# Experts' last layer as seven block products summed over the experts in PSUM, with a new order of layers and a new prologue

## The chip, the core and the metric

The kernel runs on one core of a Trainium2 chip. The metric is the device time of one execution in microseconds (us). Before the change the median of three runs was 1530.85 us (1530.27 to 1532.34). The core has five engines that matter here: PE does matmuls (PEld is its weight load), DVE and ACT do elementwise work, POOL (GpSimd) does some elementwise work and starts some transfers, and SP only starts transfers. PE writes its results to PSUM, which has eight banks of 512 numbers of four bytes for each of 128 partitions.

## The reference

The input x has 32 series of 128 steps with 256 features, that is 4096 tokens of 256. All numbers are 32-bit floats.

```python
# layer 0: attention over all 4096 tokens (8 heads of 32), masked by step
x = _L0_conv_ref(x, ...)            # h + alpha * (softmax(QK/sqrt(hd)) V @ out_w.T + out_b)
# layer 1
t = _to_tokens(x)
t = t + _L1_attn_ref(_ln_t(t), ...) # attention in a window of 24 tokens
t = t + _L1_ffn_ref(_ln_t(t), ...)
...
def _L1_ffn_ref(x, ...):
    feat = jnp.mean(x, axis=0)
    w = jax.nn.softmax(feat @ Wr + br, axis=-1)          # one share per token and expert
    h = jnp.einsum('bfd,edh->bfeh', x, W1) + b1
    h = jax.nn.relu(_bn(h, g1, be1, m1, v1))
    h = jnp.einsum('bfeh,ehk->bfek', h, W2) + b2
    h = jax.nn.relu(_bn(h, g2, be2, m2, v2))
    y = jnp.einsum('bfeh,ehd->bfed', h, Wo) + bo
    return jnp.einsum('bfed,fe->bfd', y, w)              # sum of 8 experts by their shares
```

There are 8 experts. Each has three matrices of 256x256: W1, W2 and Wo. The change concerns the product with Wo and the sum over experts.

## The kernel before, in words

`fast_kernel` has four stages in time. The prologue (to about 21 us) loads and transposes weights and the first tokens, and projects queries and keys. Block attention (to about 733 us) works on scores, exponentials and their products with the values. A transition (to about 777 us) finishes the attention of the last block and does the window attention of the first tokens. The experts' stage takes the rest.

The experts' stage goes through 64 items: 8 blocks of 512 tokens, and 8 experts for each block (`work`, a list of pairs of block and expert). The tokens of a block lie transposed: features on partitions, 512 tokens along a row. For an item, `Layer(0, ...)` multiplies them by W1 and `Layer(1, ...)` by W2, each followed by a relu on ACT with a scale and a shift.

From item 3 on (`PLAIN`) a layer is not the plain product of 2x2 blocks, which takes eight products of 128x128 by 128x256. It takes seven, in the manner of Strassen and Winograd. For this the weights' sums of blocks are computed once for each expert by `weight_sums` on POOL, written to memory (`kept`) and loaded again for later items (tile `s`). The tokens' sums of blocks are computed by `token_sums` on DVE (tiles `tx` for the first layer, `th` for the second). `Layer.first` issues four of the seven products into two PSUM tiles, `a` and `q`, then copies one half of `a` to `u` on ACT (L1960) and makes three additions on DVE (L1961, L1962, L1963). `Layer.last` issues the other three products (the first of them into `a`, two into `q`), then a relu on ACT, one addition on DVE (L1976) and two more relus. Tiles of `ps_h` (four banks) hold `a` and `q` of two layers at a time.

`combine` multiplies by Wo: for half of a block, four plain matmul pairs put tokens on partitions again (tile `psy`, L1991, from a `ps_x` bank), and two DVE instructions (L1999) multiply by the token's share and add to `tokens`, the result in SBUF. When the last expert of a block has been added, the tokens are written out.

The order in the loop over items is written out by hand: first half of the first layer of item k+1, a half combine, first half of the second layer of item k, last half of that first layer, another half combine, last half of that second layer. After each of these, `insert` puts in up to three jobs of later blocks (project, normalise, turn, window attention, route, expert shares). A job is put in when a planner's clock `now`, which adds fixed costs, says that what it needs is 3.2 us old (`LATER`), and when the work already spent is behind a line of due times (`dues`, from `SPAN`).

All 4096 tokens' x are loaded and kept in SBUF from an early time; `with_bias` (L904) adds the output bias on POOL. Tile dependencies hold for whole tiles: a matmul that writes one half of a bank waits for readers of the other half as well.

In the prologue, a tile `stack` gathers eight small vectors by POOL's DMA queue (L1079), is transposed (L1111) and copied to `colT` (L1114); `wsc` (L1116) scales the query weights by one of its columns, after which mean, spread, queries and keys follow up to the first scores, `sa`.

In the transition, `three_a`, `three_b`, `one_a`, `one_b` are PSUM tiles of attention's score pool. It is closed and `ps_h` and `ps_x` are opened in its banks (`open_banks`); the first layers' plain products are at L1939.

Of the kernel before, what the change touches and what calls it, by code (L numbers as in the profile page):

```python
# [16 lines left out]
P = 128  # L17
# [806 lines left out]
def fast_kernel(ctx: ExitStack, tc: tile.TileContext, ins: dict, out: bass.AP, narrow):  # L824
# [101 lines left out]
    with ExitStack() as l0:  # L926
# [73 lines left out]
        def project_q(b, g, hT, ps):  # L1000
# [3 lines left out]
            for c in range(2):  # L1004
# [6 lines left out]
            nc.vector.tensor_tensor(  # L1011
                qv, qv, cq[:, g, :].unsqueeze(1).to_broadcast([P, BLK // N, N]), op=ALU.add
            )
# [41 lines left out]
        with tc.tile_pool(name="pw", bufs=1) as pw, tc.tile_pool(  # L1055
            name="ptr", bufs=8, space=PSUM
        ) as ptr:
            def banks(name, n):
# [11 lines left out]
            nc.gpsimd.memset(onesm, 1.0 / D)  # L1070
            xblk[0] = load_x(0, "xg", (
                lambda: nc.scalar.dma_start(out=wQ_n, in_=in_w[0]),
                lambda: nc.scalar.dma_start(
                    out=wq_n, in_=ins["L0_conv_wq"].rearrange("(c p) d -> p c d", p=P)
                ),
# [33 lines left out]
            for c in range(2):  # L1109
                ps = ptr.tile([P, BLK], F32, tag="tr", name=f"ps_st{c}")  # L1110
                nc.tensor.transpose(  # L1111
                    ps[:, : NROW + N], stack[:, c * P : (c + 1) * P], ident[: NROW + N, : NROW + N]
                )
                nc.vector.tensor_copy(colT[:, c, :], ps[:, : NROW + N])  # L1114
            for ci in range(2):
                nc.scalar.mul(wsc[:, ci, :], pswc[ci], colT[:, ci, 0:1])  # L1116
            hT = transposed_x(0, banks("pst0", 2))
            for ci in range(2):
                nc.vector.tensor_copy(wraw[:, ci, :], pswc[ci])
            for i in range(TPB):  # L1120
                stats(0, i, xblk[0])
            transposed(wKT, wk_n, "ps_wK", banks, True)
# [6 lines left out]
            for ci in range(2):  # L1129
                nc.vector.tensor_tensor(wcT[:, ci, :], wsc[:, ci, :], ps, op=ALU.subtract)  # L1130

# [8 lines left out]
            def query_bias(g):  # L1140
# [10 lines left out]
                )  # L1151

            query_bias(0)
# [5 lines left out]
            project_q(0, 0, hT, banks("psq0_0", 1)[0])  # L1159
            project_k(0, 0, hT, banks("psk0_0", 1)[0])  # L1160
# [68 lines left out]
        with ExitStack() as at:  # L1229
# [4 lines left out]
            ps_a = scores_ps.enter_context(tc.tile_pool(name="ps_a", bufs=1, space=PSUM))  # L1234
            ps_b = scores_ps.enter_context(tc.tile_pool(name="ps_b", bufs=2, space=PSUM))
            ps_av = scores_ps.enter_context(tc.tile_pool(name="ps_av", bufs=1, space=PSUM))
# [285 lines left out]
    res = ctx.enter_context(tc.tile_pool(name="res", bufs=1))  # L1522
# [7 lines left out]
    ps_h = ps_x = None  # L1530

    def open_banks():
        nonlocal ps_h, ps_x
        scores_ps.close()
        ps_h = ctx.enter_context(tc.tile_pool(name="ps_h", bufs=4, space=PSUM))
        ps_x = ctx.enter_context(tc.tile_pool(name="ps_x", bufs=4, space=PSUM))
# [8 lines left out]
    w12, s12, wo, kept_sums = {}, {}, {}, {}  # L1545
# [15 lines left out]
    def load_last(k):  # L1561
        wo[k] = wf.tile([P, 2, D], F32, tag="wo", name=f"wo_{k}")
        expert_weights(wo[k], "Wo", work[k][1])

    def weight_sums(e):

        t = s12[e] = wf.tile([P, 4, 2, P], F32, tag="s12", name=f"s12_{e}")
        a11, a21, a12, a22 = (
            w12[e][:, :, c, m * P : (m + 1) * P] for c in range(2) for m in range(2)
        )  # L1570
        for k, (p, q, op) in enumerate((
            (a21, a22, ALU.add), (t[:, 0], a11, ALU.subtract),
            (a11, a21, ALU.subtract), (a12, t[:, 1], ALU.subtract),
        )):
            nc.gpsimd.tensor_tensor(t[:, k], p, q, op=op)
        kept_sums[e] = wdr.tile([P, 4, 2, P], F32, name=f"kept{e}")
        nc.sync.dma_start(out=kept_sums[e], in_=t)

    Ksb = l1c.tile([P, 2, D], F32, name="Ksb")
    nc.sync.dma_start(out=Ksb, in_=ins["L1_attn_K"].rearrange("(c p) e -> p c e", p=P))  # L1580
    load_tokens(4, res.tile([P, TPB, D], F32, name="tokens4"))
# [14 lines left out]
    def load_rest():  # L1596
        load_tokens(TPB + 1, res.tile([P, TPB, D], F32, name=f"tokens{TPB + 1}"))
        load_layers(1)
        for b in range(TPB + 2, NBLK):
            load_tokens(b, res.tile([P, TPB, D], F32, name=f"tokens{b}"))  # L1600
# [30 lines left out]
    def project(n):  # L1631
        ps = bank(f"pso{n}")[:, :D]
        for c in range(2):
            project_half(n, c, ps, not c)
        finish(n, ps)
        if n + TPB < NTILE:
            with_bias(n + TPB)
# [157 lines left out]

    def expert_tokens(b, r2):
# [40 lines left out]
    def turn_route(b):  # L1837
# [3 lines left out]
        wide = fx.tile([P, TPB, HD], F32, tag="w", name=f"w{b}")  # L1841
        nc.gpsimd.memset(wide, 0.0)
# [20 lines left out]
    def turn_shares(b):  # L1863
        ps = bank(f"pswt{b}")[:, :P]
        nc.tensor.transpose(ps, blk[b]["wide"].rearrange("p r e -> p (r e)"), ident)
        blk[b]["wT"] = fx.tile([P, P], F32, tag="wT", name=f"wT{b}", bufs=1)
        nc.vector.tensor_copy(blk[b]["wT"], ps)
# [38 lines left out]
    def token_sums(x, tag, name):  # L1906

        t = fh.tile([P, 4, HB], F32, tag=tag, name=name)
        nc.vector.tensor_tensor(
# [3 lines left out]
        nc.vector.tensor_tensor(t[:, 2], x[:, 1, HB:], t[:, 0], op=ALU.subtract)  # L1913
        nc.vector.tensor_tensor(t[:, 3], x[:, 1, :HB], t[:, 2], op=ALU.subtract)
# [8 lines left out]
    class Layer:  # L1923


        def __init__(self, l, k, x, t):
            self.l, self.k, self.x, self.t = l, k, x, t
            self.w, self.s = w12[k][:, l], None if t is None else s12[k][:, :, l]

        def bank(self, m):  # L1930
            return ps_h.tile([P, 2, HB], F32, tag="h", name=f"psh{self.l}_{self.k}_{m}")

        def product(self, ps, w, x, start):
            nc.tensor.matmul(ps, lhsT=w, rhs=x, start=start, stop=True, skip_group_check=True)  # L1934

        def plain(self, m):
# [6 lines left out]
            relu(self.out[:, m, :], ps, self.l, work[self.k][1], m)  # L1943

        def first(self):
            x, t, w, s = self.x, self.t, self.w, self.s
            self.out = fh.tile([P, 2, BLK], F32, tag=f"h{self.l}", name=f"h{self.l}_{self.k}")
# [6 lines left out]
            self.product(a[:, 0], w[:, 0, :P], x[:, 0, :HB], True)  # L1954
# [517 lines left out]
```

## Time and profile before

| | us |
|---|---|
| median of 3 runs | 1530.85 |
| profiled execution | 1529.69 |
| its span, first to last instruction | 1527.6 |
| experts' stage (777 to the end) | 750.6 |
| PE busy / DVE / ACT / POOL | 1477.8 / 1199.8 / 938.0 / 164.7 |
| PE busy from 1400 to 1520 | 119.14 of 120 |

The granted clock of PE was 0.996 over the span, and 0.90 between 777 and 800 us. The page's rows that the change touches most (line, engine, operation, tiles, count, busy us, mean ns of one, idle time of the engine ahead of them):

```profile
L1991 PE MATMUL psy<-wo,h 128*128 128x256 f32 x1024 | 242.9, 380 | 0.0
L1999 DVE SCALAR_TENSOR_TENSOR tokens<-psy,w,tokens 128x256 f32<-128x256 f32 x256 | 111.0, 475 | 34.9 <-PE psy L1991 34.5
L1934 PE MATMUL psh<-tx,s 128*128 128x256 f32 x366 | 89.3, 380 | 0.0
L1976 DVE TENSOR_TENSOR h<-psh,u 128x512 f32<-128x512 f32 x122 | 83.0, 681 | 1.5 <-PE psh L1934 1.4
```

A row is read so: 512 matmuls by Wo show as 1024 records, two for each; records overlap, so their sum is more than the time they take, and the pitch from one matmul to the next has to be read from a timeline.

### The profile page before, as it was taken

What the parts mean: (1) busy time and instruction counts of PE and PEld (TensorE: products, weight loads), DVE (VectorE), ACT (ScalarE), POOL (GpSimd) and SP (SyncE); (2) the same over time, 40 slices, a digit from 0 to 9 for tenths busy, and PEclk for the clock granted to TensorE, in tenths of its full rate; (3) what the DMA queues carried; (4) which work ended last, traced back from release to release, by engine and by line L of the source; (5) the groups of instructions that cost most, each with busy time, mean ns of one, the idle gap of its engine ahead of it and who ended that gap; (6) DMA issues with size and microseconds to landing.
All of it is one profiled execution on the core that took longest, in us unless ns stands there. A gap on an engine that the chain in (4) does not pass through costs nothing.

```text
span 1527.6 us, 23827 instructions
## 1 busy us (share of the span) xinstructions
PE 1477.8 (97%) x8873; PEld 836.2 (55%) x8873; DVE 1199.8 (79%) x2193; ACT 938.0 (61%) x1400; POOL 164.7 (11%) x387
## 2 busy tenths in 40 slices
PE   8999999999999999999989999999999999999998
PEld 5333232222222222222547878887877888888887
DVE  4677879888899898999737777687877877777775
ACT  4676777878888887988545345445454444544443
POOL 2110003000000000031062103001010000000000
PEclk9999999999999999999999999999999999999999
DMA  5211101010000010000323334433433333343442
GB/s 127 48 43 26 29 8 31 8 30 8 1 15 8 2 49 15 8 9 1 116 81 106 103 118 126 127 111 107 130 113 115 123 107 119 119 130 110 138 152 64
DMA packets 96106, 110.16 MB, mean 72 GB/s; under 512 B 17677, under 2 KB 84960, under 8 KB 95984
## 3 DMA queue, kind: packets, MB, share of 16 engines
q1 hardware_dynamic: 93280, 106.87, 23.2%
q8 instruction: 72, 1.18, 0.3%
q0 software_dynamic: 1888, 0.91, 0.2%
q10 hardware_dynamic: 816, 0.79, 0.2%
q14 instruction: 50, 0.41, 0.1%
HBM read 98.87 MB, written 8.53 MB: 70 GB/s over the span
## 4 chain that ended last, share of the span: by engine, by line
PE 75%; DVE 12%; ACT 7%; issue 4%; POOL 1%; DMA 0%; DVEq 0%; ACTq 0%; POOLq 0%
PE psh L1934 18%; PE sa L1271 15%; PE av L1315 14%; PE psy L1991 11%; DVE acc L1305 3%; ACT h L1919 2%; PE psv L1020 2%; PE psq L1005 2%; ACT pt L1285 2%; PE psk L992 2%; PE psk L1685 2%; PE sb L1271 1%; PE sums L1342 1%; PE psh L1939 1%; DVE h L1976 1%
## 5 line engine op out<-in xcount | busy, mean ns | idle before, releaser
L1305 DVE TENSOR_TENSOR acc<-acc,pt 128x1024 f32<-128x1024 f32 (+3 forms) x500 | 529.3, 1126 | 40.6 <-ACT pt L1285 28.4
L1285 ACT ACTIVATE pt<-sb 128x1536 f32<-128x1536 f32 (+3 forms) x288 | 387.3, 1345 | 3.8 <-PE sb L1271 3.6
L1271 PE MATMUL sa<-q,kT 32*128 32x512 f32 (+3 forms) x576 | 302.3, 604 | 9.4 <-ACT pt L1283 7.1
L1271 PE MATMUL sb<-q,kT 32*128 32x512 f32 (+3 forms) x1728 | 306.8, 605 | 1.8 <-ACT pt L1285 0.7
L1919 ACT ACTIVATE h<-h,bshift,bscale 128x256 f32<-128x256 f32 x244 | 159.2, 699 | 228.8 <-DVE h L1976 228.8
L1315 PE MATMUL av<-pt,v 128*32 128x512 f32 (+3 forms) x2304 | 287.0, 571 | 1.5 <-ACT big_t L1330 0.4
L1991 PE MATMUL psy<-wo,h 128*128 128x256 f32 x1024 | 242.9, 380 | 0.0
L1283 ACT ACTIVATE pt<-sa 128x512 f32<-128x512 f32 (+3 forms) x288 | 162.5, 564 | 94.5 <-PE sb L1271 63.1
L1991 PEld LDWEIGHTS psy<-wo,h 128*128 128x128 f32 x1024 | 191.9, 190 | 30.7 <-issue 5.8
L1271 PEld LDWEIGHTS sa<-q,kT 32*128 32x128 f32 x576 | 84.3, 183 | 220.7 <-ACT pt L1283 179.5
L1315 PEld LDWEIGHTS av<-pt,v 128*32 128x32 f32 x2304 | 45.5, 108 | 200.7 <-issue 183.4
L1999 DVE SCALAR_TENSOR_TENSOR tokens<-psy,w,tokens 128x256 f32<-128x256 f32 x256 | 111.0, 475 | 34.9 <-PE psy L1991 34.5
L1961 DVE TENSOR_TENSOR u<-psh,u 128x256 f32<-128x256 f32 x122 | 51.0, 418 | 101.3 <-ACT u L1960 101.0
L1289 POOL MEMSET pt<- 32x128 f32 (+2 forms) x192 | 58.5, 305 | 631.6 <-ACT pt L1285 536.1
L1919 ACT ACTIVATE h<-psh,bshift,bscale 128x256 f32<-128x256 f32 (+1 forms) x132 | 75.9, 575 | 54.7 <-PE psh L1934 41.5
L1960 ACT COPY u<-psh 128x256 f32<-128x256 f32 x122 | 44.2, 362 | 80.3 <-PE psh L1934 80.2
L1271 PEld LDWEIGHTS sb<-q,kT 32*128 32x128 f32 x1728 | 88.1, 183 | 9.1 <-ACT pt L1285 5.8
L1934 PE MATMUL psh<-tx,s 128*128 128x256 f32 x366 | 89.3, 380 | 0.0
L1934 PE MATMUL psh<-th,s 128*128 128x256 f32 x366 | 88.9, 379 | 0.0
L1976 DVE TENSOR_TENSOR h<-psh,u 128x512 f32<-128x512 f32 x122 | 83.0, 681 | 1.5 <-PE psh L1934 1.4
L1934 PEld LDWEIGHTS psh<-tx,s 128*128 128x128 f32 x366 | 69.2, 190 | 10.4 <-DVE h L1976 0.8
L1934 PEld LDWEIGHTS psh<-th,s 128*128 128x128 f32 x366 | 69.5, 190 | 9.5
(329 smaller groups left out, 1771.0 us busy)
## 6 DMA issues: line engine op xcount, KB each, us to landing
w<-in_L_ffn_W_dram SPq DMA_DIRECT2D x128, 256.0 KB
s<-kept SPq DMA_DIRECT2D x56, 512.0 KB
wo<-in_L_ffn_Wo_dram SPq DMA_DIRECT2D x64, 256.0 KB
xg<-in_x_dram SPq DMA_DIRECT2D x32, 128.0 KB
tokens<-in_x_dram SPq DMA_DIRECT2D x8, 512.0 KB
kept<-s SPq DMA_DIRECT2D x8, 512.0 KB
out_dram<-tokens SPq DMA_DIRECT2D x32, 128.0 KB
rec<-flat SPq DMA_DIRECT2D x60, 64.0 KB
```

The costliest lines, as they stand in the source:

```text
L1271: nc.tensor.matmul((sb[:, h - 1, :] if h else sa)[:, lo:], lhsT=kT[rows, g, j * P : (j + 1) * P], rhs=q[rows, g, lo:], start=True, stop=True,)
L1283: nc.scalar.activation(pt[:, 0, lo:], sa[:, lo:], AF.Exp, scale=SCALE)
L1285: nc.scalar.activation(pt[:, 1:, lo:], sb[:, :, lo:], AF.Exp, scale=SCALE)
L1289: nc.gpsimd.memset(pt[k * N : (k + 1) * N, :, lo : lo + k * N], 0.0)
L1305: nc.vector.tensor_tensor(live[b, g][:, hs, lo:], old[:, hs, lo:], pt[:, hs, lo:], op=ALU.add)
L1315: nc.tensor.matmul(av[h * HD : (h + 1) * HD, lo:], lhsT=v[:, j, (g * HG + h) * HD : (g * HG + h + 1) * HD], rhs=pt[:, h, lo:], start=(j == ...
L1919: nc.scalar.activation(dst, src, AF.Relu, bias=bshift[:, m, k : k + 1], scale=bscale[:, m, k : k + 1])
L1934: nc.tensor.matmul(ps, lhsT=w, rhs=x, start=start, stop=True, skip_group_check=True)
L1961: nc.vector.tensor_tensor(u, a[:, 1], u, op=ALU.add)
L1976: nc.vector.tensor_tensor(flat.rearrange("p (k c) -> p k c", k=2), self.q, self.u.unsqueeze(1).to_broadcast([P, 2, HB]), op=ALU.add,)
L1991: nc.tensor.matmul(ps[:, i, :], lhsT=ht[:, c, r * P : (r + 1) * P], rhs=wo[k][:, c, :], start=(c == 0), stop=(c == 1),)
L1999: nc.vector.scalar_tensor_tensor(out=tokens(n), in0=ps[:, i, :], scalar=w[:, r, e : e + 1], in1=tokens(n), op0=ALU.mult, op1=ALU.add,)
```

## The change

The product with Wo is made in seven block products as well, for all items but the first two and the last two (`SUMMED`). The token's share is multiplied into the second layer's output beforehand, so that the products of all experts of a block can be added in PSUM; the sum over experts is then a sum over matmuls into the same four banks (`ps_y`), with features on partitions. For this:

- `turn_shares` writes the block's shares to memory, and `load_shares` loads one expert's shares as a row spread over all partitions (tile `wb`). `shared` multiplies the layer's output by it and makes the block sums `ty`, all on POOL.
- `last_sums` makes the sums of Wo's blocks on DVE once for each expert, and keeps them in memory.
- `last_products` is a generator that issues the seven products one at a time. After a block's last expert `close_block` adds the banks up (one copy on ACT, six additions on DVE), and `turn_out` transposes the result back, adds it to the tokens and writes two tiles at a time.
- `ps_h` and `ps_x` have two banks each in place of four.
- The order of the loop: first half of a layer, `between`, last half of the same layer, `between`. `between` issues up to two of the waiting products (when the planner's clock passes `SHARED` or `SUMS` after the second layer) and one costed job, with another after the second product. The four first products go in the order a0, a1, q0, q1; the relu of the rows' second half is issued only after the next layer's copy of u (`rest`).
- Tokens of the later four blocks are loaded when an earlier block's are out (`load_again`), with the bias as a job; squares for a check of bounds are formed in place.
- The pools of the transition open in another order (`ps_a`, `ps_av`, `ps_b`).
- In the prologue `wsc` is scaled by a column loaded on its own (`lng`), some transposes and the first key projection come earlier, and one addition of the query bias later.

The core of the diff:

```diff
-        ps_h = ctx.enter_context(tc.tile_pool(name="ps_h", bufs=4, space=PSUM))
-        ps_x = ctx.enter_context(tc.tile_pool(name="ps_x", bufs=4, space=PSUM))
+        ps_h = ctx.enter_context(tc.tile_pool(name="ps_h", bufs=2, space=PSUM))
+        ps_x = ctx.enter_context(tc.tile_pool(name="ps_x", bufs=2, space=PSUM))
+        ps_y = ctx.enter_context(tc.tile_pool(name="ps_y", bufs=1, space=PSUM))
...
             self.product(a[:, 0], w[:, 0, :P], x[:, 0, :HB], True)
+            self.product(a[:, 1], s[:, 1], t[:, 2], False)
             self.product(q[:, 0], s[:, 0], t[:, 0], True)
-            self.product(a[:, 1], s[:, 1], t[:, 2], False)
             self.product(q[:, 1], s[:, 2], t[:, 1], False)
...
+    def shared(k):
+
+        b, e = work[k]
+        wb = blk[b].pop(("wb", e))
+        for c in range(2):
+            nc.gpsimd.tensor_tensor(h2[k][:, c, :], h2[k][:, c, :], wb, op=ALU.mult)
+        return h2[k], token_sums(h2[k], "ty", f"ty{k}", nc.gpsimd)
+
+    def last_products(k):
...
+        y, w, s = ys[b], wo[k], so[k]
+        x, t = h2t[k]
+        for i, j, lhs, rhs in (
+            (0, 0, w[:, 0, :P], x[:, 0, :HB]), (0, 1, w[:, 1, :P], x[:, 1, :HB]),
+            (1, 0, s[:, 3], x[:, 1, HB:]), (1, 1, s[:, 0], t[:, 0]),
+            (2, 1, s[:, 2], t[:, 1]), (2, 0, s[:, 1], t[:, 2]),
+            (3, 0, w[:, 1, P:], t[:, 3]),
+        ):
...
+            nc.tensor.matmul(
+                y[i][:, j], lhsT=lhs, rhs=rhs, start=first, stop=True, skip_group_check=True
+            )
+            yield
...
+    SHARED, SUMS = 6.5, 9.2
...
+        if not forced and now < second_done[k] + (SHARED if i < 3 else SUMS):
+            return False
...
+    def between():
+        if not product() and plain_halves:
+            combine(*plain_halves.pop(0))
+            passed(1.73)
+        insert()
+        if to_load:
+            begin_shared()
+        if product():
+            insert(True)
...
+    def begin(layer, t=1.73):
+        nonlocal done
+        layer.first()
+        if done:
+            done.rest()
+        done = None
+        passed(t)
...
-    SPAN = E * 9.5
+    SPAN = E * 9.05
...
-        dues.append((SPAN * b - 40, dues[-1][1] + share[b]))
+        dues.append((SPAN * b - 45, dues[-1][1] + share[b]))
...
+            begin(one)
+            begin_shared()
...
+            if k:
+                between()
+            end(one)
+            between()
...
+        begin(two)
...
+        between()
+        end(two)
         h2[k] = two.out
+        second_done[k] = now
+        between()
...
             for ci in range(2):
+                nc.scalar.mul(wsc[:, ci, :], pswc[ci], lng[:, ci : ci + 1])
+                nc.vector.tensor_copy(wraw[:, ci, :], pswc[ci])
```

## The prediction

> **What bounds the kernel now.** I read the page's busy table first, then busy time by window, then the timeline of one late item, then the chain that ended last at the two joints of the program. In the tables below the columns after the window are its length and the busy time of PE, PEld, DVE, ACT and POOL, then granted clock, DMA share and GB/s.
>
> ```profile
> PE 1477.8 (97%) x8873; PEld 836.2 (55%) x8873; DVE 1199.8 (79%) x2193; ACT 938.0 (61%) x1400; POOL 164.7 (11%) x387
> ...
> 1460.82:1470.32 9.50, 9.50 (x46) 8.36 (x45) 6.75 (x15) 4.26 (x9) 0.00 (x0) 1.00 0.42 138
> 1470.32:1479.82 9.50, 9.50 (x46) 8.36 (x45) 6.75 (x15) 4.26 (x9) 0.00 (x0) 1.00 0.45 141
> ```
>
> Each of these windows is one item of the experts' stage, and PE has no gap in it. An item is two layers of seven products and a combine of eight matmuls, 22 matmuls of 128x256; each shows as two records, and 9.50 / 22 gives a pitch of 0.432 us. So here a matmul taken away is 0.432 us gained, provided that the ones left do not start to wait. Whether they do is read from the chain inside a layer (start, duration, what; the order of these lines is PE, then ACT, then DVE):
>
> ```profile
> 1475.12 0.59 PE L1934 MATMUL psh<-h,w 128*128 128x256 f32 x2
> 1475.56 1.46 PE L1934 MATMUL psh<-th,s 128*128 128x256 f32 x6
> ...
> 1476.62 0.38 ACT L1960 COPY u<-psh 128x256 f32<-128x256 f32 x1 [1.46 <-PE psh L1934]
> ...
> 1475.20 0.43 DVE L1961 TENSOR_TENSOR u<-psh,u 128x256 f32<-128x256 f32 x1 [1.63 <-ACT u L1960]
> 1475.73 0.42 DVE L1962 TENSOR_TENSOR h<-psh,u 128x256 f32<-128x256 f32 x1
> 1476.19 0.42 DVE L1963 TENSOR_TENSOR h<-psh,h 128x256 f32<-128x256 f32 x1
> ```
>
> The copy of u begins 1.50 us after the layer's first product (1475.12 to 1476.62): a1 is the third product, issued at 0.86 with a record pair of 0.59, and the copy follows its end by 0.05. From the start of a copy to the end of the last of the three adds takes 1.79 us (a copy at 1474.82, L1963 ending at 1476.61). Only then may the layer's second half write the q bank again. Now four products of the other layer and a half combine always stand in between, so this chain is hidden: all waits of psh on L1963 together are 1.7 us.
>
> The joint between attention and experts is the one place with a plain hole in PE:
>
> ```profile
> 771.31 0.86 PE one_a L1886 x4
> 772.17 0.62 PE three_a L1829 x16
> ...
> 776.15 0.32 DVE tokens L1640
> 776.48 0.25 issue
> 776.72 3.75 PE psh L1939 x4
> 780.47 0.21 PE psrt L1839
> 780.68 2.19 PE psh L1939 x4
> ```
>
> PE stops at about 772.7 and begins again at 776.72, 3.98 us later, when DVE has added the last of four projections held in bank three_b. The next four records (two 128x512 matmuls) take 3.75 us; the same work at full clock takes 1.73 to 2.19. At the start, the chain runs through a load:
>
> ```profile
> 4.16 6.20 DMA stack<-in_L_conv_sym_emb_dram
> 10.36 0.14 issue
> 10.49 0.24 PE ps_st L1111
> 10.76 0.21 DVE colT L1114
> 10.99 0.48 ACT wsc L1116
> ...
> 21.41 0.66 PE sa L1271
> ```
>
> Everything up to the first scores at 21.41 hangs on that landing at 10.36.
>
> **The change, part by part.** Counts are from the two programs' instruction orders.
>
> 1. PE work. Sixty of 64 items lose their combine: 480 matmuls x 0.432 = 207.4 us off. They gain seven block products each: 420 x 0.432 = 181.4 us on. Turning the sums back costs 64 transposes of 128x128 at 0.108 (the pitch of such a transpose in this trace), 6.9 us. Net **-19.1 us**. A dense item becomes 21 x 0.432 = 9.07 us. DVE loses 240 additions of 475 ns (L1999), 114 us, and gains about six operations per block; nothing waits for DVE's total, so both count as nothing by themselves. The cover is that DVE is busy 6.75 of 9.50 us in the late items; what of it lies in a chain is counted in part 2.
>
> 2. Two PSUM banks for a layer in place of four. The four new accumulators take banks from both pools. Two layers can no longer be open at once, so the order becomes first half, filler, second half of the same layer. With a1 now second, the copy can start at 0.43 + 0.59 + 0.05 = 1.07, the adds end at 1.07 + 1.79 = 2.86, and the second half's q product may start at about 2.91. Dense, it would start at 5 x 0.432 = 2.16 plus the filler. The wait is therefore 0.75 us less the filler, never below nothing. In the new order 18 second layers have no filler (12 of them among items 44 to 62), and seven more have 0.11 to 0.65 us. That is 18 x 0.75 + (0.64 + 4 x 0.53 + 0.32 + 0.10) = **+16.7 us**. First layers have 0.86 or more and count nothing; their cover is two of the new products. A late item then takes 9.82 us against 9.50 now. Bounds: 8 us if half of the chain turns out shorter than these starts say, 22 us if DVE is 0.3 us late each time, as at the copy of 1476.62, whose add began only at 1477.31.
>
> 3. ACT and DVE bursts on that chain. A block's jobs put four normalisations (0.59 us each, 2.4 in all) into ACT's queue, ahead of some u copy; before, a whole half combine hid that. Seven blocks x 2.4 = 17 us if all is exposed, nothing if the filler at the point hides it. Fillers where jobs stand are mostly 0.86 and more, so I take a third, **+6 us** (0 to 17). The relu of the second half's rows, 0.8 us, moves behind the next copy of u; who waits for it is the GpSimd sums of part 5.
>
> 4. First block. The other pool also has two banks, so bias and transpose jobs that now run ahead wait for the tile two before them. The nearest rows are waits of 0.3 to 1.0 us of job matmuls (psbo 0.3, psrt 0.6, pswt 0.8); some six such places give **+3 us** (0 to 6).
>
> 5. GpSimd. It is idle in the late items and gets, for each item, two multiplications and one sum of 128x512 (1.05 us, as L2018) and two sums of 128x256 (0.73): 4.6 us of 9.1. It can start some 2.2 us after the item's first matmul, when the deferred relu is done, and is done by 6.8; the planner asks for the first product at 7.2 and for the sums at 9.9. So the matmuls do not wait: 0, with 3 us of cover. If that cover went, each us late would be 60 us of PE.
>
> 6. DMA. Each item gets a share row of 256 KB and sums of 256 KB, beside 1.25 MB now; the DMA share of 0.42 to 0.45 becomes about 0.62 (0.44 x 1.75 / 1.25). The issues are on SP, which has no compute; weights are requested two items (19 us) ahead. I take 0; a load late by 1 us would stop PE by as much.
>
> 7. The joint. The new order of pools gives psh banks that ACT's relu frees at 773.0 instead of DVE's additions at 776.5. Gain 776.72 - 773.0 = 3.7 us, and 1.8 us more if the first matmuls keep the full clock (3.55 us from 776.72 to 780.27, against 1.73): **-5.5 us** (-3.5 to -5.5). The four additions then run under the matmuls.
>
> 8. Prologue. The scale no longer waits for the large stack but for a row loaded on its own, and key projection moves ahead. Walking the chain with the trace's durations, the first scores come at 19.2 to 21.4; PE's own work of 8 projections and transposes keeps the gain small. **-1.5 us** (0 to -2.2).
>
> 9. One costed job per point. PE's waits at job matmuls in this stage (psp on L1727 2.8 us, psa 0.8, pswt 0.8, psr, psf and psrt 0.6 each, psh 1.7) sum to 7.9 with psbo excepted; spreading jobs may remove half: **-4 us** (0 to -8).
>
> Sum: -19.1 + 16.7 + 6 + 3 - 5.5 - 1.5 - 4 = **-4.4 us**. On the profiled execution, 1529.69 us, that is 1525.3; it lies 1.16 us under the median of 1530.85, so the median forecast is **1526**.
>
> A row that bears on part 5: of DVE's tiny additions with both inputs in SBUF some last far longer than others.
>
> ```profile
> L1721 DVE TENSOR_TENSOR nm<-nm,negt x32: 158/158/1045, 755.1 to 1365.8; 128x1 f32<-128x1 f32 x32
> ```
>
> The long ones lie under GpSimd additions, while additions with one input in PSUM, such as L1962, show no difference (425 ns). [...]
>
> In the new order th starts some 7.6 us after the item's first matmul and GpSimd has finished at 6.8, so I add nothing; if they met, one operation of 1.05 us in 60 items would put up to 63 us into DVE's queue ahead of the adds of part 2.
>
> **The rivals.** A, the PE gain comes through: the chain of part 2 costs 8 instead of 16.7, the bursts cost 0: -4.4 - 8.7 - 6 = -19, **1511**. For it speaks that L1963 hardly ever shows as a releaser of PE now; against it, that this is due to filler which is gone in 18 layers.
> B, slower: the same chain, but longer by x in every layer, because ACT's or DVE's queue holds something before the u copy (a relu of 0.55, the close of a block). The 25 second layers with little filler pay x each, and some 60 layers with 0.86 to 1.08 of filler pay x - 0.15. At x = 0.3 that is 7.5 + 9 = 16.5 us more: **1542**. It turns from faster to slower at x of about 0.17. For it: a copy at 1474.82 now begins 1.7 us after its input, behind two relus. Against: the new order moves the longest relu out of the way.
> C, GpSimd or the th sums are late (parts 5 and 6), 0.5 us in each of 60 items: 1526 + 30 = **1556**. Against it, 3 us of cover.
> D, the parts cancel and nothing is to be measured: **1531**.
>
> **How the numbers follow.** About 0.2%, 3 us, is what a measurement of this kernel can tell from no change. The forecast with its own range of 1518 to 1534 has 0.48, of which 0.12 lies within 3 us of 1530.85 and is rival D. A has 0.25, B 0.21, C 0.06. Faster: 0.36 + 0.25 = 0.61; same 0.12; slower 0.27. The range takes in most of A and B: 1507 to 1543, which leaves C and the ends of A and B out.
>
> **What would show it.** Right: PE's hole at 773 is gone; the first scores come near 19; late items last about 9.8 us, with one idle of 0.7 us per item in front of the second layer's q product, released by DVE's third add; the new products never wait for GpSimd. A shows as a late period of 9.1 to 9.3. B shows as psh waits on DVE in first layers too, with the u copy starting later than 0.05 us after a1's end. C shows as idle of the new products released by POOL, or as th sums above 0.68 us. The forecast is wrong if the late period is under 9.5 or the waits of all layers pass 26 us.

## The result, and the profile after

The changed kernel takes 1578.70 us (median of 4 runs, 1575.94 to 1583.62), against 1531.59 us for the kernel before in the same comparisons: a ratio of 1.0312 with a 95% interval of 1.0298 to 1.0326, 47 us slower. The profiled execution took 1575.94 us with a span of 1574.0 and a mean granted clock of 0.991.

The page's busy table, and busy time by window for two late items, with the columns as before:

```profile
PE 1489.5 (95%) x8817; PEld 816.5 (52%) x8817; DVE 1188.6 (76%) x2049; ACT 949.0 (60%) x1406; POOL 483.1 (31%) x681
...
1472.66:1482.65 9.99, 9.62 (x43) 7.73 (x42) 5.28 (x12) 4.49 (x8) 5.27 (x5) 1.00 0.55 184
1482.65:1492.65 10.00, 9.62 (x44) 7.74 (x43) 5.29 (x12) 4.49 (x8) 5.26 (x5) 1.00 0.59 184
```

A late item has one matmul less than before and still lasts 10.0 us instead of 9.50; PE is no longer full. PE's busy time rose from 1477.8 to 1489.5 us, although it has fewer matmuls. The four largest rows of the view of waits for PE in the experts' stage (engine, line, total us, times, longest us):

```profile
PE psh L1962 <- DVE u L1991: 15.0, 14, 2.6
PE psh L1962 <- DVE h L1993: 10.2, 33, 0.4
PE ptx L1694 <- DVE tokens L2113: 9.3, 2, 8.7
PE psh L1962 <- DVE h L2005: 6.1, 9, 1.0
```

The same view of the kernel before has 4.0 us for the joint, 2.8 for one pair of jobs and 1.7 for the third addition of a layer. So PE's four largest waits are now for DVE, and no wait of its matmuls in this stage is for POOL. L1991 is the addition to u (L1961 before), L1993 the third addition (L1963), L2005 the addition in a layer's second half (L1976), L2113 the plain combine.

**A late layer.** Timeline of one second layer of the changed kernel, PE first, then ACT, then DVE:

```profile
1487.85 0.59 PE L1962 MATMUL psh<-h,w 128*128 128x256 f32 x2
1488.28 1.46 PE L1962 MATMUL psh<-th,s 128*128 128x256 f32 x6
1489.80 0.70 PE L1962 MATMUL psh<-h,w 128*128 128x256 f32 x2
1490.82 0.70 PE L1962 MATMUL psh<-h,s 128*128 128x256 f32 x2 [0.32 <-DVE h L1993]
1491.35 0.59 PE L1962 MATMUL psh<-th,w 128*128 128x256 f32 x2
1491.78 0.59 PE L2052 MATMUL y<-h,wo 128*128 128x256 f32 x2
...
1488.91 0.37 ACT L1990 COPY u<-psh 128x256 f32<-128x256 f32 x1 [0.83 <-PE psh L1962]
...
1489.32 0.42 DVE L1991 TENSOR_TENSOR u<-psh,u 128x256 f32<-128x256 f32 x1 [1.87 <-ACT u L1990]
1489.88 0.42 DVE L1992 TENSOR_TENSOR h<-psh,u 128x256 f32<-128x256 f32 x1
1490.34 0.42 DVE L1993 TENSOR_TENSOR h<-psh,h 128x256 f32<-128x256 f32 x1
```

The copy starts 1.06 us after the layer's first product and the third addition ends at 2.91; the q product starts at 2.97. The layer, seven matmuls with nothing between, takes 3.93 us from its first product to the next matmul (1491.78) instead of 3.02: 0.91 us. Only 0.32 us of this stand in the view of waits; PE counts as busy for the rest, so the view understates such a loss.

**The start of the stage.** Timeline between 786 and 800 us, PE, POOL and DVE together in order of start:

```profile
787.07 0.27 PE L1889 MATMUL pswt<-ident,wide 128*128 128x128 f32 x1
787.47 1.03 POOL L2137 TENSOR_TENSOR rec_last<-Ksb 128x512 f32<-128x512 f32 x1
788.53 0.69 DVE L2154 TENSOR_REDUCE kss<-rec_last 128x1 f32<-128x512 f32 x1 [8.05 <-POOL rec_last L2137]
789.33 1.37 DVE L1586 TENSOR_TENSOR so<-wo 128x128 f32<-128x128 f32 x1
...
792.28 1.21 DVE L1936 TENSOR_TENSOR tx<-xfT 128x512 f32<-128x512 f32 x1
...
795.13 0.86 DVE L2113 SCALAR_TENSOR_TENSOR tokens<-psy,wide,tokens 128x256 f32<-128x256 f32 x2
...
796.05 0.69 PE L1694 MATMUL ptx<-ident,xl 128*128 128x128 f32 x2 [8.71 <-DVE tokens L2113]
796.53 3.62 PE L1706 MATMUL psk<-big_t,Ksb 128*128 128x512 f32 x4
```

DVE is idle for 8.05 us until POOL's last square is done; sums of Wo's blocks and of tokens follow, and only then DVE frees PE's bank (L2113). PE is idle for 8.71 us. The two matmuls of 128x512 that follow (four records, psk) take 3.62 us at a granted clock of 0.50; before the change eight such records took 3.60 us at 1.00.

**Closing a block.** DVE and PE around 1117 us:

```profile
1116.09 0.43 DVE L2069 TENSOR_TENSOR C<-y,C 128x256 f32<-128x256 f32 x1
1116.43 0.41 DVE L2070 TENSOR_TENSOR uv<-y,uv 128x256 f32<-128x256 f32 x1
1116.88 0.69 DVE L2072 TENSOR_TENSOR C<-y,uv 128x512 f32<-128x512 f32 x1
1117.61 0.42 DVE L2075 TENSOR_TENSOR C<-y,C 128x256 f32<-128x256 f32 x1
1117.95 0.41 DVE L2076 TENSOR_TENSOR C<-y,uv 128x256 f32<-128x256 f32 x1
1118.28 0.41 DVE L1991 TENSOR_TENSOR u<-psh,u 128x256 f32<-128x256 f32 x1
...
1118.75 0.70 PE L1962 MATMUL psh<-h,w 128*128 128x256 f32 x2 [1.77 <-DVE u L1991]
```

The copy of u was done at 1116.5; its addition waits 1.8 us behind the closing additions, and PE with it. Of the 14 waits for the u addition (15.0 us), six stand behind such a closing (7.0 us), five behind slow sums of Wo's or the tokens' blocks (5.4 us), and one of 1.98 us, before 1057 us, behind four normalisations on ACT.

### The profile page after: what moved, and what is told of

Read it like the earlier page. It is cut to its first block, busy times and chain, and to the rows that moved or that the text cites. A ratio compares the mean times of both kernels' runs of the same rounds, so it can differ in the third digit from the quotient of the medians.

```text
span 1574.0 us, 24174 instructions
## 1 busy us (share of the span) xinstructions
PE 1489.5 (95%) x8817; PEld 816.5 (52%) x8817; DVE 1188.6 (76%) x2049; ACT 949.0 (60%) x1406; POOL 483.1 (31%) x681
## 4 chain that ended last, share of the span: by engine, by line
PE 72%; DVE 16%; ACT 5%; issue 4%; POOL 2%; DMA 1%; DVEq 0%; ACTq 0%; SPq 0%; POOLq 0%
PE psh L1962 18%; PE sa L1280 14%; PE av L1324 13%; PE y L2052 9%; DVE acc L1314 2%; PE psv L1026 2%; PE psq L1005 2%; PE psk L992 2%; ACT pt L1294 2%; PE psk L1706 2%; PE sb L1280 1%; DVE h L1992 1%; DVE h L1993 1%; PE sums L1351 1%; ACT pt L1292 1%
## 5 line engine op out<-in xcount | busy, mean ns | idle before, releaser
L1946 ACT ACTIVATE h<-h,bshift,bscale 128x256 f32<-128x256 f32 x244 | 172.5, 708 | 175.5 <-DVE h L2005 175.4
L2032 POOL TENSOR_TENSOR h<-h,wb 128x512 f32<-128x512 f32 x120 | 152.2, 1275 | 305.1 <-ACT h L1946 303.9
L1991 DVE TENSOR_TENSOR u<-psh,u 128x256 f32<-128x256 f32 x122 | 51.4, 421 | 113.2 <-ACT u L1990 112.5
L2005 DVE TENSOR_TENSOR h<-psh,u 128x512 f32<-128x512 f32 x122 | 83.3, 683 | 56.7 <-PE psh L1962 56.4
L2052 PE MATMUL y<-ty,so 128*128 128x256 f32 x360 | 103.7, 383 | 0.0
L1962 PE MATMUL psh<-h,w 128*128 128x256 f32 x244 | 75.5, 391 | 10.6 <-DVE u L1991 9.6
L1962 PE MATMUL psh<-xfT,w 128*128 128x256 f32 x244 | 74.2, 386 | 6.9 <-DVE u L1991 5.4
L1936 POOL TENSOR_TENSOR ty<-h 128x512 f32<-128x512 f32 x60 | 77.0, 1284 | 4.7
```

Source lines behind the costliest of these rows:

```text
L1936: eng.tensor_tensor(t[:, 0:2], x[:, :, HB:], x[:, 0, :].rearrange("p (k c) -> p k c", k=2), op=ALU.subtract,)
L1946: nc.scalar.activation(dst, src, AF.Relu, bias=bshift[:, m, k : k + 1], scale=bscale[:, m, k : k + 1])
L2005: nc.vector.tensor_tensor(flat.rearrange("p (k c) -> p k c", k=2), self.q, self.u.unsqueeze(1).to_broadcast([P, 2, HB]), op=ALU.add,)
L2032: nc.gpsimd.tensor_tensor(h2[k][:, c, :], h2[k][:, c, :], wb, op=ALU.mult)
L2052: nc.tensor.matmul(y[i][:, j], lhsT=lhs, rhs=rhs, start=first, stop=True, skip_group_check=True)
```

## The experiments

Times below are medians; e, c, f, g and p kernels are edits of the changed kernel, b kernels of the kernel before, which took 1530.5 to 1531.3 in each group.

**e1_rows: one reduction later.**

```diff
-            job("bound_rows", 0, bound_rows, ("square", "K"))
+            job("bound_rows", 0, bound_rows, ("square", "K"), ("columns", "wK"))
```

> Only the place of the job bound_rows is changed (it waits for the column sums of wK as well, so DVE's reduction of GpSimd's last square is issued some 16 us of planner time later). Theory (the startup hole of 8.7 us in front of ptx at 787 us, and the half-clock stretch after it, come from DVE standing behind GpSimd's squares): 9 to 12 us faster than the changed kernel, 1567 to 1570 us, and PE busy from 787 on. Rival (GpSimd's queue is late by itself, so that PE or DVE then waits for something else of GpSimd): less than 3 us.

1564.65 us, 14.0 faster than the changed kernel. The wait at ptx went from 8.7 to 0.9 us, while the waits for the u addition rose from 15.0 to 18.3. The mean granted clock of the profiled run rose from 0.991 to 0.997, which helps to make the gain larger than the hole; part of that rise looks like chance, as the last section shows.

**e2_close: closing additions behind the chain.** `close_one` issues the next waiting group, after a layer's first half and after its last.

```diff
-        if last and i in (1, 5, 6):
-            close_block(b, i)
+        if last and i == 1:
+            close_block(b, 1)
+        elif last and i in (5, 6):
+            to_close.append((b, i))
...
         layer.first()
...
+        close_one()
```

> Only the order on DVE is changed: the six additions that close a block are issued in two groups, each behind a layer's own chain and not ahead of it; the next block's first product is let in 2.2 instead of 4 planner us after the close. Theory (PE waits for the u addition that stands behind these additions, 5 holes of 0.5 to 1.7 us, 5.5 us in all, with a slow-clock stretch behind the longest): 5 to 9 us faster than the changed kernel, about 1571. Rival (the additions only move the wait, to L2005 and the next layer's q): 0 to 2 us.

1585.63 us, 7 slower: a miss, and worse than the rival. PE's waits for the u addition fell only from 15.0 to 13.6 us, those for L2005 rose from 6.1 to 11.8 and those for L1993 from 10.2 to 12.0. Moving the additions, and letting the next block in earlier, also changed the order of the matmuls behind them, so this run does not price the closing.

**e3_shared: products admitted earlier.**

```diff
-    SHARED, SUMS = 6.5, 9.2
+    SHARED, SUMS = 5.5, 9.2
```

> Only the constant SHARED is changed, 6.5 to 5.5, so that two products stand in the second layer's gap in most late items; second layers with an empty gap fall from 17 to 7. Theory (the two-bank chain costs 0.9 us for each empty gap, as the late period of 9.99 us shows): about 10 to 12 us faster than the changed kernel, about 1567, late periods of 9.07 to 9.2 us. Rival (GpSimd's shares are not ready that early): less than 4 us, with PE idle in front of y released by POOL.

1560.07 us, 18.6 faster. The late items that got their products last some 9.25 us. Ten gaps of 0.91 explain half of the gain; the rest was not traced to one place.

**e4_sums: Wo's block sums on POOL.**

```diff
-        block_sums(nc.vector, t, *(
+        block_sums(nc.gpsimd, t, *(
```

> Only the engine of the sums of Wo's blocks is changed, DVE to GpSimd, 32 operations of 128x128 in the first block. Theory (on DVE these have two inputs in SBUF and stand under GpSimd's additions, 0.28 us alone but up to 1.37 us there, and hold up the u addition, 4.1 us of holes and a slow-clock stretch at 860 us): 4 to 7 us faster than the changed kernel, about 1573. Rival (GpSimd then brings the shares later, and the products wait for it): no gain, up to 3 us slower.

1565.68 us, 13.0 faster, more than twice the middle of what was expected, although POOL got more to do. Part of it is e1's hole, which falls from 8.7 to some 6.3 us here, and the waits for the u addition fall from 15.0 to 11.1.

**c1_three: the three together.**

> The changed kernel with the edits of e1_rows, e3_shared and e4_sums together. Theory (three separate waits in front of PE): their gains add up, 14.0 + 18.6 + 13.0 = 45.6 us, less some 3 us in the first block where e1 and e4 shorten the same hole: 1534 to 1540 us, about the time of the kernel before the change. Rival (one shared cause, so that each edit gets much of the same gain): over 1548.

1543.86 us: 34.8 of the 45.6 us. So there is not one shared cause, but the gains overlap by 11 us, more than I allowed. Some of this overlap can be the clock: the changed kernel's profile has two stretches at half clock (0.50 for 3.4 us each), behind 1057 and 1119 us, and the profiles of e1_rows, e3_shared and e4_sums each lack both, though the last two have one elsewhere.

**c2_norm: one normalisation at a time.**

```diff
+            if name[0] == "normalise" and normed:
+                k += 1
+                continue
```

> c1_three, and at most one normalisation per insertion point in place of four, so that ACT's queue holds 0.6 and not 2.1 to 2.4 us ahead of the copy of u. Theory (one hole of 1.9 us at 1055 us with a slow-clock stretch behind it, and smaller ones): 2 to 5 us faster than c1_three. Rival (the four are hidden by filler nearly everywhere): within 2 us.

1547.91 us, not faster than c1_three (ratios to before 1.0129, 1.0098 to 1.0160, against 1.0088, 1.0072 to 1.0105). Spreading the burst on ACT gains nothing, but it also delays jobs, so that the price of the burst alone stays open.

**p1_nopool: the item's work on POOL left out.**

```diff
-        for c in range(2):
-            nc.gpsimd.tensor_tensor(h2[k][:, c, :], h2[k][:, c, :], wb, op=ALU.mult)
-        return h2[k], token_sums(h2[k], "ty", f"ty{k}", nc.gpsimd)
+        return h2[k], ys["ty"]
```

> The changed kernel without GpSimd's work for each item: the multiplication by the shares and the block sums of the second layer's output are left out, and the last products use one constant tile in place of the sums. PE's, DVE's and ACT's instructions and their order are as in the changed kernel. [...] Rival (GpSimd's work for the items is what made the change slow): 30 us faster and more, close to the kernel before.

1558.50 us, 20.2 faster: more than the 4 to 12 us that were expected, less than the rival's 30. No matmul of the changed kernel's experts' stage waited for POOL, and the order on PE, DVE and ACT is the same, so this is what POOL cost through DVE, but for some 3 us that may be clock (by the estimate of the last section). The busy table:

```profile
PE 1482.6 (95%) x8817; PEld 818.9 (53%) x8817; DVE 1154.5 (74%) x2049; ACT 948.8 (61%) x1406; POOL 165.1 (11%) x382
```

The same 2049 instructions on DVE take 34.1 us less, and PE's waits for L1991, L1993 and L2005 fall from 15.0, 10.2 and 6.1 to 9.8, 8.0 and 3.2 us. Late items, in which DVE has no jobs, last 9.96 us against 9.99: the gain lies where jobs are. One line of the tile view shows the stretch, for the changed kernel and then for p1_nopool (minimum, median and maximum in ns):

```profile
L1936 DVE TENSOR_TENSOR tx<-xfT x8: 683/1124/1253, 792.3 to 1423.4; 128x512 f32<-128x512 f32 x8
```

```profile
L1936 DVE TENSOR_TENSOR tx<-xfT x8: 656/680/1206, 790.0 to 1405.4; 128x512 f32<-128x512 f32 x8
```

Before the change this was 673/681/684.

**f1_fill and f2_tx: SHARED at 4.5, and the token sums on POOL.**

```diff
-    SHARED, SUMS = 5.5, 9.2
+    SHARED, SUMS = 4.5, 9.2
...
-        blk[b]["t"] = token_sums(blk[b]["xfT"], "tx", f"tx{b}")
+        blk[b]["t"] = token_sums(
+            blk[b]["xfT"], "tx", f"tx{b}", nc.gpsimd if b else nc.vector
+        )
```

> c1_three with SHARED at 4.5 in place of 5.5: second layers with an empty gap fall from 7 to 2. Theory (0.9 us for each empty gap): 4 to 5 us faster than c1_three, about 1539. Rival (the shares are not ready that early): not faster, with y released by POOL.

1542.87 us, within the runs' spread of c1_three: five more filled gaps gave nothing clear.

> f1_fill with the block sums of the tokens (tx, seven blocks) on GpSimd in place of DVE. Theory (two waits of 0.9 and 2.8 us for a u addition that stands behind tx, which DVE makes in 2.6 us while GpSimd works and in 1.5 alone, with a slow-clock stretch behind the longer): 3 to 6 us faster than f1_fill. Rival (2.7 us more in GpSimd's queue makes the shares late, so products wait): no gain.

1534.84 us, 8.0 faster than f1_fill, again more than the two waits named. It is the best form of the changed kernel that was found: it wins back 43.9 of the 47 us with POOL's work for the items still in place, and is still 1.0025 (1.0014 to 1.0037) of the kernel before.

**g1_six and g2_six: half of the closing moved, and the next block let in earlier.**

```diff
-        if last and i in (1, 5, 6):
+        if last and i in (1, 5):
             close_block(b, i)
+        elif last and i == 6:
+            to_close.append((b, i))
```

> f2_tx with one of the two groups of additions that close a block, the last three (1.5 us), issued on DVE behind the next layer's own chain and not ahead of it. Matmul order and fillers are those of f2_tx. Theory (three waits of 1.1 us for a u addition behind these groups, and the waits for the third addition that follow them): 3 to 5 us faster than f2_tx, 1530 to 1532, no difference from the kernel before. Rival (as in e2_close, the additions hold up L2005 in place of the u addition): within 2 us of f2_tx or slower.

> g1_six with the next block's first product let in 1.5 in place of 4 planner us behind the close; no layer then has an empty gap (two in g1_six). Theory: 1.5 to 3 us faster than g1_six, just faster than the kernel before, 1527 to 1531. Rival (the first product then waits for the additions that read its bank, as long as the gap was): no faster than g1_six.

1535.64 and 1542.73 us. g1_six does not differ from f2_tx, and g2_six, whose only other edit lets the next block in 1.5 instead of 4 planner us after the close, is 7.9 slower. Both miss. That the closing additions hold up something wherever they stand on DVE is the likely reason, which these runs do not show.

**b1_pools, p2_pools and b4_joint: the joint.** b1 has the new order of pools without the small ones, p2 the small ones with the old order, b4 both on the kernel before:

```diff
-        ps_h = ctx.enter_context(tc.tile_pool(name="ps_h", bufs=4, space=PSUM))
+        ps_h = [
+            ctx.enter_context(tc.tile_pool(name=f"ps_h{l}", bufs=2, space=PSUM)) for l in range(2)
+        ]
```

> The kernel before with one part of the change alone, the order of the attention's PSUM pools (ps_a, ps_av, ps_b). Theory (step 7 of the prediction): PE's hole of 3.98 us at 773 us is gone and the matmuls behind it keep the clock, 3.5 to 5.5 us faster than before, 1526 to 1528. Rival (the first matmuls then wait for something else, or the jobs behind lose their cover): less than 2 us.

> The changed kernel with the attention's PSUM pools in the order of the kernel before (ps_a, ps_b, ps_av). Theory (step 7: the order gives the first psh the banks that are free early): 3.5 to 5.5 us slower than the changed kernel, 1582 to 1584, with the hole at 773 us back. Rival (it is the size of ps_h, two banks in place of four, that lets the first psh start): within 2 us of the changed kernel, no hole.

> The kernel before with the order of the attention's pools changed (as b1_pools) and ps_h as two pools of two banks, one for each layer, in place of one pool of four. Order of work and number of banks are as before. Theory (a pool waits for all that lies in its banks: the order alone, b1_pools, and the small pool alone, p2_pools, kept the hole, both together remove it): the hole of 3.98 us is gone and the matmuls behind keep the clock, 4 to 5.5 us faster than before, 1525.5 to 1527. Rival (the first psh still waits): within 2 us of the kernel before.

b1_pools took 1531.01 us (1.0001, 0.9991 to 1.0010): no gain, the hole is there as before. p2_pools took 1581.96, 3.3 over the changed kernel, with the hole back. b4_joint took 1527.71, 0.9982 (0.9972 to 0.9991) of the kernel before: 2.8 us faster, less than the 4 to 5.5 expected, and the fastest kernel of this study. Its joint (timeline of PE):

```profile
773.67 0.64 PE L1831 MATMUL three_a<-xfT,Wr 128*32 128x128 f32 x16
774.61 1.98 PE L1941 MATMUL psh<-xfT,w 128*128 128x512 f32 x4 [0.29 <-ACT h L1921]
778.18 0.30 PE L1841 MATMUL psrt<-ident,lgT 128*128 128x128 f32 x1 [1.59 <-DVE tokens L1642]
```

In the three runs together the first product waits only 0.29 us when its pool is both small and opened over the new order, and 3.98 us with either alone. That fits a pool that waits for all that lies in its banks. Here 1.59 us then come back at the next pool.

**b2_two, b3_quarter and b5_rest: two banks alone.** On the kernel before, two banks for layers and for jobs and the new order of layers. b2 keeps the half combines between a layer's halves; b3 spreads quarters over all four places; b5 also moves the last relu behind the next copy of u.

```diff
+            if not i:
+                yield
...
             one.first()
+            if k:
+                two.rest()
```

> The kernel before with two PSUM banks in each of the two pools and with the changed order of layers and products (first half, half combine, last half of one layer, then the other layer; a0, a1, q0, q1), but with its combine as before. Theory (two banks cost only where the filler between the halves of a layer is short; here it is 1.73 us or more everywhere): 1529 to 1536 us, within 5 us of the kernel before. Rival (two banks cost by themselves): 1545 us and more.

> The kernel before with two banks for the layers, two for the jobs and four for its combine, the changed order of layers and products, and a quarter of an item's combine (0.86 us of PE) in each of the four places: between the halves of each layer and behind each layer. It has no GpSimd work for the items, no block closing and no shares. Theory (two banks are nearly free where each of the four places has 0.86 us of filler, so b2_two was slow for want of filler between the layers): 1533 to 1548 us. Rival (two banks cost far more than the empty gaps, through the hand-over of banks to a DVE that is late): 1560 us and more.

> b3_quarter with the last relu of a layer's output issued behind the next layer's copy of u (the changed kernel's rest). Theory (in b3_quarter the copy starts at 1.48 us and not 1.06 behind two relus, so each layer waits 0.31 us in spite of 0.86 us of filler, 0.62 us for each item of 10.12): some 30 to 38 us faster than b3_quarter, 1532 to 1540, late items of 9.50 us, so that two banks cost next to nothing. Rival (the wait is DVE's load, not ACT's order): within 10 us of b3_quarter.

1681.33, 1570.39 and 1550.04 us; the first two miss and the third is 20 faster than b3_quarter where 30 to 38 were expected. In b2_two PE waits 56 times (62.1 us) for the previous layer's second addition (L1976), 48 of them in first layers, where nothing stands between the layers. A late first layer of b3_quarter, PE, then ACT, then DVE:

```profile
1489.50 0.59 PE L1935 MATMUL psh<-xfT,w 128*128 128x256 f32 x2
...
1492.09 0.59 PE L1935 MATMUL psh<-xfT,w 128*128 128x256 f32 x2
1492.83 0.70 PE L1935 MATMUL psh<-xfT,s 128*128 128x256 f32 x2
...
1489.77 1.31 ACT L1920 ACTIVATE h<-h,bshift,bscale 128x256 f32<-128x256 f32 x2 [1.44 <-DVE h L1977]
1490.98 0.35 ACT L1961 COPY u<-psh 128x256 f32<-128x256 f32 x1
...
1492.35 0.42 DVE L1964 TENSOR_TENSOR h<-psh,h 128x256 f32<-128x256 f32 x1
```

The copy starts 1.48 us after the first product, behind two relus; the chain ends 0.3 us too late for 0.86 us of filler, twice for each item of 10.12 us. With the relu moved, late items take 9.53 us: two banks then cost nothing there. b5_rest is still some 20 us slower than the kernel before, without any of POOL's new work. This was lost in the earlier items, where jobs stand in the queues, and was not followed further.

## Why the prediction was wrong

It expected 1526 us; 47 us of loss came in place of 5 of gain. The step that failed is step 5, GpSimd at "0", and with it the sentence of step 1 that nothing waits for DVE's total: POOL's work slowed DVE, DVE's queue held up PE, and p1_nopool prices this at 20.2 us. Steps 4 and 2 were mis-sized beside it. The steps are the numbered parts of the prediction.

- **Step 1, PE work: the count right, the cover wrong.** PE's records fell by 56, as counted, and a filled late item comes down to 9.25 us in e3_shared, near 9.07. But DVE's six closing operations, counted as nothing, stand ahead of the u addition six times, 7.0 us in all.
- **Step 2, empty gaps: the mechanism right, the size too small.** A layer without filler costs 0.91 us, not 0.75: the matmul behind a wait starts the next one 0.10 us later (1490.82 to 1491.35, 0.53 instead of 0.432), and the first product of the second half also waits, for the u addition. Late items take 9.99 us where 9.82 were forecast. The prediction counted 18 empty gaps; with the small matmuls of jobs counted as filler there are 17. That makes 15.5 us in place of 13.5, a small miss. What two banks and the new order cost in the earlier items had no term; b5_rest, some 20 us slower than the kernel before with them and without POOL's work, points to one.
- **Step 3, bursts: put on the wrong engine.** One hole of 1.98 us stands behind normalisations on ACT, and c2_norm could gain nothing by spreading them. DVE's queue was the place: in the changed kernel PE waits 21 us in all for L1991 and L2005.
- **Step 4, first block: mis-sized.** It was put at 3 us from job waits of 0.3 to 1.0 us. The start holds a wait of 8.7 us; e1_rows gives 14.0 us back, some of it clock. The cause is a job without cost: the planner admits all of these at once, and this one put a DVE reduction behind POOL's queue. The instruction order showed it, but I walked only PE's and not DVE's.
- **Step 5, GpSimd "0": the step that failed.** I asked whether PE would wait for POOL, found 3 us of cover, and its matmuls never did. I did not ask what POOL would do to DVE while it works: p1_nopool puts that at 20.2 us, and e4_sums and f2_tx gain 13.0 and 8.0 by taking additions from DVE, although POOL gets them. The reason for adding nothing, that th starts when POOL is done, holds in late items (th: median 681 ns, as before) and was carried over to the first blocks, to tx and to Wo's sums, which start at any time. The row of nm that the prediction shows was the warning: such additions come with every block's jobs.
- **Step 6, DMA: right.** The share rose to 0.55 to 0.59 in late items and PE has no wait of note for a load.
- **Step 7, the joint: too large, and wrong in cause.** The first product comes at 772.47 instead of 776.72, but p2_pools prices the joint at 3.3 us and b4_joint at 2.8, below the 3.5 to 5.5 stated. And the order alone, which the step named, gains nothing (b1_pools).
- **Step 8, prologue: rather too small.** The first scores come at 18.73 us, a little earlier than walked. In this profile only 0.64 us of that are left at the joint (router matmuls at 771.53 against 772.17), but it has one stretch of 3.4 us at half clock more near 160 us (6.8 us at a granted clock of 0.50, against 3.4 before). Over the profiles of all forms, the router matmuls start at 768.7 to 771.5 us (median 769.6) in the thirteen with the new prologue and at 772.1 to 773.9 (median 773.3) in the six with the old one.
- **Step 9, one job per point: not seen.** Beside the 9.3 us at ptx, waits of job matmuls still sum to some 7.8 us in the view of waits; before they summed to 6.5 without psh.

The prediction's own sign of being wrong came: the waits of the layers are 15.0 + 10.2 + 6.1 = 31.3 us, over its 26. Of the rivals B was nearest in mechanism (waits in first layers too, and the close of a block ahead of the u addition) and C in time; neither had DVE held up by POOL. C's sign, new products released by POOL or slow th sums, hardly came: no new product's matmul waited for POOL, and th took 869 ns at most.

The account is not a ledger. e1_rows, e3_shared and p1_nopool gain 14.0, 18.6 and 20.2 us, which happens to be the distance between forecast and result, but the forecast already held 16.7 us for the gaps, and c1_three shows that such gains overlap. How much the closing and the two banks cost by themselves stays open.

## What to carry to other kernels

Work given to an idle engine is not free because nobody waits for it: list which instructions of its neighbours run at the same time, see in a trace which of them last longer beside it (here tx, 1124 ns instead of 681), and price those. When filler is taken out of a dense PE stream, walk the chain that it hid on every engine's queue, with what stands ahead in that queue, and give each place where the banks change hands its own filler. A job whose cost a planner counts as zero still has a place in a queue; it needs a limit as well.

## What the runs showed of the hardware

In these runs DVE instructions with two inputs in SBUF took longer while POOL worked on SBUF. The 128x128 sums of Wo took 273 to 1368 ns (the median of their first form 284), and tx 1124 instead of 681. The plainest case is nm, an addition of one number per partition, here in the changed kernel and then in p1_nopool:

```profile
L1742 DVE TENSOR_TENSOR nm<-nm,negt x32: 159/168/1195, 754.4 to 1372.7; 128x1 f32<-128x1 f32 x32
```

```profile
L1742 DVE TENSOR_TENSOR nm<-nm,negt x32: 158/158/560, 752.1 to 1357.0; 128x1 f32<-128x1 f32 x32
```

In the changed kernel 14 of the 32 took over 0.25 us, and each of these ended 0.01 to 0.02 us after the end of a POOL instruction. In p1_nopool it is one. An example, with the u addition that stands behind it:

```profile
1301.19 1.27 POOL L2032 TENSOR_TENSOR h<-h,wb 128x512 f32<-128x512 f32 x1 [5.66 <-ACT h L1946]
1301.29 1.20 DVE L1742 TENSOR_TENSOR nm<-nm,negt 128x1 f32<-128x1 f32 x1
...
1302.40 0.41 DVE L1991 TENSOR_TENSOR u<-psh,u 128x256 f32<-128x256 f32 x1
```

Additions with one input in PSUM did not change: u took 392/424/426 ns, and 391/424/426 before. The longest nm, tx and Wo sums lost 0.57 to 1.08 us, less than one POOL operation of an item (1.26 us or more). xf, a TENSOR_SCALAR with one tensor input, took longer too, in the tile view of the changed kernel, where it had been 397/405/415 before:

```profile
L1829 DVE TENSOR_SCALAR xf<-tokens,mean,rstd x32: 381/413/1420, 762.9 to 1412.8; 128x256 f32<-128x256 f32 x32
```

POOL's instructions took longer at times as well, though seldom: its 128x256 sums of ty (L1941) took 727 ns in the median and up to 1212. Its 128x512 operations on two different inputs took 1.26 us or more each time; the prediction's 1.05 us came from squares, which have one input. An item is 5.3 us of POOL, not 4.6.

Behind some short holes of PE the granted clock was 0.50 for a while; the length of a hole does not tell which. Windows of 2 us behind the hole of 1.77 us at 1117 (the third number from the end is the granted clock):

```profile
1116.00:1118.00 2.00, 0.98 (x5) 0.52 (x3) 1.90 (x6) 1.08 (x2) 0.00 (x0) 1.00 0.00 0
1118.00:1120.00 2.00, 0.93 (x3) 0.53 (x4) 1.83 (x6) 0.45 (x1) 0.00 (x0) 0.88 0.00 0
1120.00:1122.00 2.00, 2.00 (x5) 1.61 (x6) 1.28 (x4) 0.11 (x1) 0.00 (x0) 0.50 0.00 0
1122.00:1124.00 2.00, 2.00 (x9) 1.11 (x8) 0.61 (x2) 0.60 (x1) 0.72 (x1) 0.77 0.00 0
```

The clock is 0.50 for about 3.4 us (0.5 us of the second window, all of the third, 0.9 us of the fourth), so by this estimate the hole costs nearly as much again. Behind the holes of 1.98 and 2.60 us at 1055 and 861 it was 0.50 for 3.4 us too; at that of 1.61 us at 1220 the clock stayed at 1.00. Other runs have the same holes with another outcome. In e1_rows the hole of 1.98 us, here from 1044.58 to 1046.56, left the clock alone, and so did that of 1.77:

```profile
1044.00:1046.00 2.00, 0.58 (x3) 0.18 (x1) 0.00 (x0) 2.00 (x6) 1.77 (x4) 1.00 0.06 18
1046.00:1048.00 2.00, 1.12 (x4) 0.70 (x5) 1.75 (x4) 1.32 (x3) 1.84 (x5) 1.00 0.15 37
```

In e4_sums both were harmless and the hole of 1.61 us halved the clock; c1_three kept its clock through 2.85 us, and p1_nopool lost it behind 1.47. Between these two lengths it looks like chance.

One minus the granted clock, times the span, is the author's upper estimate of what the clock cost: 16.6 us in the mean of the four runs of the changed kernel and 6.8 to 8.3 us in the groups of the kernel before. For p1_nopool it is 13.6 us. By this estimate up to some 9 of the 47 us are clock, and small differences between single edits can be luck with it.
